# Column groups of 32 in the convolutions, and layer 0's B and C by way of DMA, in a four-layer image kernel

## The chip, the core and the metric

The kernel runs on one core of a Trainium2 chip. The metric is the device time of one execution in microseconds (us); the time before is the median of three runs. A profile of one further execution stands beside it.

## What is computed

The input is a batch of 4 images of 96 channels and 128 x 128 pixels, float32. Four layers follow one another, each as `x = x + layer(group_norm(x))`, with group norms over 32 groups of 3 channels:

- **Layer 0**: a 1x1 projection and a depthwise 3x3 convolution with SiLU give `u`; a second projection gives a gate `z`. Two selective scans with one state each (forward and backward over all 16384 pixels) run over `u`:

```
x_dbl = einsum('bkcl,kdc->bkdl', xs, x_proj_w)      # 6 rows for dt, one for B, one for C
delta = softplus(einsum('bkrl,kcr->bkcl', dts, dt_proj_w) + dt_proj_b)
h = exp(delta*A) * h + delta * u * B ;  y = h * C   # along the pixels
```

  Their sum is normed over the channels, gated with `silu(z)` and projected.
- **Layer 1**: a gated 3x3 convolution of 32 channels, a fractional Fourier path and a Fourier path of 32 channels each, then a dense 3x3 convolution over 96 channels.
- **Layer 2**: a deformable 3x3 convolution: offsets and masks by a 3x3 convolution, then four neighbours gathered for each pixel and tap.
- **Layer 3**: a mask, a 2-D cosine transform, four Mamba blocks (one for each quadrant, 192 inner channels, 16 states), and the transform back.

## The kernel before

**Stages.** For each image there is a *front* (layers 0 and 1 and the offsets of layer 2), a *back* (gathers and sampled convolution of layer 2, head and transform of layer 3), and *layer 3* proper (the scans), then the inverse transform. In time: the front of image 0 alone; then for each image b a stage in which the back of b runs beside the front of b+1 (and beside the inverse transform of b-1), followed by layer 3 of b alone; the last image has its back without a front. Three stages hold both a back and a front.

**Two lanes in one program.** In these stages a planner (class `Program`) records every operation of both lanes and issues them in an order that it works out from costs of its own (`cost`). Each lane is first tried alone (`measure`); an operation's due time there, divided by the lane's length, is its key, and among operations that could start at nearly the same time the lower key goes first. All are issued through one helper, so all their engine instructions stand at line 65 in the profile and their DMAs at line 408. The attribute `pace` scales due times: layer 0's scan sets `self.program.pace = 0.1`, so that this stretch takes up a tenth of its length in the keys, and layer 1 sets it back to 1. Each engine runs its instructions in the order issued, and nearly all DMAs are issued from one queue, SyncE's (SP).

**Layer 0 and layer 1's last convolution** work on blocks of 16 rows (2048 pixels; 8 blocks). `conv9` makes one chunk of 512 pixels: 9 taps, each a float32 matmul of 96 channels in, 96 out, 512 columns, summed in one PSUM tile (tile names `l_pc<-rows,l_wc` in layer 0, `l_p<-rows,l_c` in layer 1). The profile shows each float32 matmul as two MATMUL records. A block is four chunks; in layer 0 each chunk has a tenth matmul, the gate's (`l_pz<-rows,l_winT`). `u` and `silu(z)` go to DRAM planes.

**Layer 0's scan** makes 64 steps an image (32 chunks, two directions). One step: load `uc`; matmul `pd` (delta's argument, `wd`); ACT abs, relu, exp, ln and a DVE add (`l_dl`); matmul `pB` with `wbc`, whose columns all repeat the B row, so that B stands on all 96 partitions of PSUM; ACT exp (`l_dA`); DVE `du = uc * pB`; POOL `du * dl`; DVE scan (`l_h`); matmul `pC` in the same way; DVE `h * pC`. In the second half of the steps there follow the sum of both directions, norm, gate and projection (five more matmuls).

**The back's gathers**: 1152 indirect DMAs an image from POOL (`l_g<-quad_d,l_i`), 128 pixels of 1536 bytes each; each is weighed by two ACT and two DVE operations (`l_sm`, `l_part`), then transposed and multiplied.

**Layer 3** has its order written by its own list scheduler (class `Order`, with costs and keys given by hand). An image is 16 tiles of 48 scans (128 partitions x 512). For each scan: ACT `dA`; matmul `pB` and DVE `dB = du * pB` (one scan of four has its product `dP` from POOL instead, out of lines that a DMA spreads, `l_cl`); DVE scan `l_h`; POOL `hc = h * C` (cost 1.23 in the list); matmul `py` that sums `hc` in PSUM. Each tile has a head: norm, convolution `pu` and gate `pz` (192 channels of two quadrants laid over three tiles of 128; the middle tile, j = 1, holds 64 rows of each quadrant and so takes two matmuls with 64 output columns each), projections, softplus. `T.xq` takes its three leading columns from the tile before, by a DVE copy.

Of the kernel before, what the change touches and what calls it, by code (L numbers as in the profile page):

```python
# [22 lines left out]
F32 = mybir.dt.float32  # L23
# [9 lines left out]
L = H * W  # L33
# [100 lines left out]
class Tile:  # L134


    def __init__(self, shape, make, kind, real=None):
        self.shape, self.make, self.kind, self.real = shape, make, kind, real
        self.ops, self.reads, self.writes = [], [], []
# [58 lines left out]
class Pool:  # L198
# [19 lines left out]
    def tile(self, shape, dtype, name, tag=None, bufs=None):  # L218
        tag = tag or name
        tile = Tile(shape, lambda: self.pool.tile(shape, dtype, name=name, tag=tag, bufs=bufs), self.kind)  # L220
        tiles = self.tags.setdefault(tag, [])
        tile.before = tiles[-1] if tiles else None
        n = bufs or self.bufs
        tile.slot = tiles[-n] if len(tiles) >= n else None
        tiles.append(tile)
        return View(tile)
# [10 lines left out]
class Program:  # L237
# [88 lines left out]
    def touch(self, op, view, write):  # L326
# [11 lines left out]
        t.ops.append(op)  # L338
        p0, p1, f0, f1 = view.region()
# [19 lines left out]
    def cost(self, engine, name, out, ins):  # L359
# [7 lines left out]
        if engine == "PE":  # L367
            return 1.1 * (0.00085 * n if name == "transpose" else max(0.165, 0.005 + 0.001667 * n)), None
# [139 lines left out]
class Net:  # L508
# [32 lines left out]
    def stats_tile(self):  # L541
        return self.small.tile([C, NCH, 6], F32, name="stats", tag="stats", bufs=(1, 3)[self.program.lane])
# [37 lines left out]
    def conv9(self, ps, wt, src, i, g):  # L580
# [3 lines left out]
        r0 = BR * i + 4 * g  # L584
        taps = [(0, 0)] + [(y, x) for y in (-1, 0, 1) for x in (-1, 0, 1) if (y, x) != (0, 0)]
        for n, (y, x) in enumerate(taps):
            ra, rb = max(r0, -y), min(r0 + 4, H - y)
            ca, cb = max(0, -x), min(W, W - x)
            at = ra + y - BR * i + 1
            self.nc.tensor.matmul(  # L590
                out=p3[:, ra - r0 : rb - r0, ca:cb],
                lhsT=wt[:, (y + 1) * 3 + x + 1, :],
                rhs=s3[:, at : at + rb - ra, ca + x : cb + x],
                start=n == 0,
                stop=n == 8,
            )
            if n % 3 == 2:
                yield 2.6
# [22 lines left out]
    def layer0(self, xin, T, beside):  # L621
        nc, a = self.nc, self.a
        u_d, sz_d, part_d = self.plane("u_d"), self.plane("sz_d"), self.plane("part_d")
        st0, T.st1 = self.stats_tile(), self.stats_tile()
        with self.program.pool(name="l0w", bufs=1) as wp, self.program.pool(name="l0p", bufs=1, space=PSUM) as ps:
# [6 lines left out]
            nc.sync.dma_start(out=xpd, in_=a["L0_conv_x_proj_w"][:, 0:R6, :].rearrange("k r c -> r k c"))  # L632
            wc = wp.tile([C, 9, C], F32, name="l0_wc")
# [22 lines left out]
            wd = wp.tile([C, 2, C], F32, name="l0_wd")  # L656
            wbc = wp.tile([C, 4, C], F32, name="l0_wbc")
            for k in range(2):
# [3 lines left out]
                nc.vector.tensor_copy(wd[:, k, :], pw[:C, :C])  # L662
                for n in range(2):
                    nc.vector.tensor_copy(
                        wbc[:, 2 * k + n, :], xpT[:, k, R6 + n : R6 + n + 1].to_broadcast([C, C])
                    )
# [3 lines left out]
            with self.program.pool(name="l0a", bufs=3) as wa, self.program.pool("l3i", 2) as wt:  # L670

                def block(i):
# [5 lines left out]
                    for g in range(4):  # L678
                        s = slice(BR * i * W + g * CH, BR * i * W + (g + 1) * CH)
                        pc = ps.tile([C, CH], F32, name="l0_pc", tag="a", bufs=2)  # L680
                        yield from self.conv9(pc, wc, xb, i, g)
                        u = wa.tile([C, CH], F32, name="l0_u", tag="u")
                        nc.scalar.activation(u, pc, AF.Silu, bias=v[:, 0:1], scale=1.0)
                        nc.sync.dma_start(out=u_d[:, s], in_=u)
                        pz = ps.tile([C, CH], F32, name="l0_pz", tag="b", bufs=1)
                        nc.tensor.matmul(
                            out=pz, lhsT=winT[:, C : 2 * C], rhs=xb[:, W + g * CH : W + (g + 1) * CH],
                            start=True, stop=True,
                        )
                        yield  # L690
                        sz = wa.tile([C, CH], F32, name="l0_sz", tag="sz")
                        nc.scalar.activation(sz, pz, AF.Silu)
                        nc.sync.dma_start(out=sz_d[:, s], in_=sz)

                jobs = [staggered((block(i) for i in range(NB)), 16)]
# [3 lines left out]
            self.program.pace = 0.1  # L699
            with self.program.pool(name="l0b", bufs=3) as wb:  # L700
                edges = [None, None]

                def scan(k, n):
                    t = n if k == 0 else NCH - 1 - n
                    s = slice(t * CH, (t + 1) * CH)
                    uc = wb.tile([C, CH], F32, name="l0_uc", tag="uc", bufs=6)
                    nc.sync.dma_start(out=uc, in_=u_d[:, s])
                    second = n >= NCH // 2
                    if second:
                        xc = wb.tile([C, CH], F32, name="l0_x", tag="x", bufs=4)  # L710
                        nc.sync.dma_start(out=xc, in_=xin[:, s])
                        sz = wb.tile([C, CH], F32, name="l0_z", tag="z", bufs=4)
                        nc.sync.dma_start(out=sz, in_=sz_d[:, s])
                    yield
                    yield
                    pd = ps.tile([C, CH], F32, name="l0_pd", tag="b", bufs=1)
                    nc.tensor.matmul(out=pd, lhsT=wd[:, k, :], rhs=uc, start=True, stop=True)
                    yield
                    dl = wb.tile([C, CH], F32, name="l0_dl", tag="dl")
                    tmp = wb.tile([C, CH], F32, name="l0_tmp", tag="tmp")  # L720
# [6 lines left out]
                    pB = ps.tile([C, CH], F32, name="l0_pB", tag="c", bufs=2)  # L727
                    nc.tensor.matmul(out=pB, lhsT=wbc[:, 2 * k, :], rhs=uc, start=True, stop=True)
# [4 lines left out]
                    nc.vector.tensor_tensor(du, uc, pB, ALU.mult)  # L733
# [18 lines left out]
                    if second:  # L752
                        part = self.load(wb, part_d[:, s], [C, CH], "l0_part", 3)
                    pC = ps.tile([C, CH], F32, name="l0_pC", tag="c", bufs=2)
                    nc.tensor.matmul(out=pC, lhsT=wbc[:, 2 * k + 1, :], rhs=uc, start=True, stop=True)
                    yield
                    nc.vector.tensor_tensor(h, h, pC, ALU.mult)
# [13 lines left out]
                    sq = wb.tile([C, CH], F32, name="cn_s", tag="sq")  # L771
# [4 lines left out]
                    nc.tensor.matmul(out=pv, lhsT=self.cavg, rhs=sq, start=True, stop=True)  # L776
                    yield
                    nc.scalar.activation(sq, pv, AF.Ln, bias=self.eps[:C], scale=1.0)
                    nc.scalar.activation(sq, sq, AF.Exp, scale=-0.5)
                    yield  # L780
                    nc.vector.tensor_tensor(ct, ct, sq, ALU.mult)
# [15 lines left out]
    def layer1(self, T):  # L797
        nc, a = self.nc, self.a
        self.program.pace = 1.0
# [4 lines left out]
        T.st2 = self.stats_tile()  # L804
        with self.program.pool(name="l1w", bufs=1) as wp:
# [13 lines left out]
            cb = self.load(wp, a["l1_vec"], [C, 2], "l1_cb")  # L819
            cb0 = wp.tile([64, 1], F32, name="l1_cb0")  # L820
            for j in range(2):
# [13 lines left out]
            with self.program.pool(name="l1p", bufs=2, space=PSUM) as ps, self.program.pool(  # L835
# [49 lines left out]
                def block(i):  # L885
# [22 lines left out]
                    for g in (0, 2):  # L908
                        at = BR * i * W + g * CH
                        pc = ps.tile([64, 4, W], F32, name="l1_pc", tag="c", bufs=1)  # L910
                        for n, x in enumerate((0, -1, 1)):
                            ca, cb_ = max(0, -x), min(W, W - x)
                            nc.tensor.matmul(
                                out=pc[:, :, ca:cb_], lhsT=w0s[:, x + 1, :],
                                rhs=x4[:, 2 * g : 2 * g + 4, 0, ca + x : cb_ + x],
                                start=n == 0, stop=n == 2,
                            )
                        yield
                        c0 = wm.tile([64, 4, W], F32, name="l1_c0o", tag="c0", bufs=3)
                        nc.scalar.activation(c0, pc, AF.Identity, bias=cb0, scale=1.0)  # L920
                        to = cat_d[0:32, at : at + 8 * W].rearrange("o (r two w) -> o r two w", two=2, w=W)
                        for j in range(2):
                            nc.sync.dma_start(out=to[:, :, j, :], in_=c0[32 * j : 32 * j + 32])
                        yield
                        yield
# [25 lines left out]
            with self.program.pool(name="l1r", bufs=2, space=PSUM) as ps, self.program.pool(name="l1c", bufs=3) as wa:  # L951

                def block2(i):
# [3 lines left out]
                    for g in range(4):  # L957
                        t = 4 * i + g
                        s = slice(t * CH, (t + 1) * CH)
                        xc = self.load(wa, T.x1[:, s], [C, CH], "l1_x")  # L960
                        pc = ps.tile([C, CH], F32, name="l1_p2", tag="a")
                        yield from self.conv9(pc, w2, xb, i, g)
                        nc.vector.scalar_tensor_tensor(xc, pc, cb[:, 1:2], xc, ALU.add, ALU.add)
                        nc.vector.bn_stats(T.st2[:, t, :], xc)
                        nc.sync.dma_start(out=T.x2[:, s], in_=xc)

                yield from staggered((block2(i) for i in range(NB)), 12)
# [745 lines left out]
    def pair_head(self, i, at, T, before, wq, wb, ps, order):  # L1713
# [12 lines left out]
        def load():  # L1726
# [8 lines left out]
            else:  # L1735
                nc.vector.tensor_copy(T.xq[:, :, 0:3], last.xq[:, :, CH : CH + 3])

        o("DVE", 0.2, load, "load",
# [64 lines left out]
        def conv(j, k, q, p, n, ch, first):  # L1803
            if first:
                v.pu[j] = ps.tile([128, CH], F32, name="l3_pu", tag="a")
            nc.tensor.matmul(
                out=v.pu[j][p : p + n, :], lhsT=T.wts[1][:, q, k, ch : ch + n],
                rhs=T.xq[:, q, k : k + CH], start=k == 0, stop=k == 3,
            )

        def gate(j, q, p, n, ch, first):
            if first:
                v.pz[j] = ps.tile([128, CH], F32, name="l3_pz", tag="a")
# [537 lines left out]
```

## Time and profile before

| | |
|---|---|
| median of 3 runs | 15512.11 us (15500.95 to 15518.31) |
| the profiled execution's own time | 15515.38 us |
| its span, first to last instruction | 15513.2 us |
| busy: PE, DVE, POOL, ACT | 84%, 73%, 69%, 58% |
| front of image 0, alone | 0 to 1443 us |
| back 0 with front 1; back 1 with front 2; back 2 with front 3 | 1443 to 3548; 5074 to 7168; 8652 to 10806 |
| layer 3 of images 0, 1, 2, 3 | 3548 to 5074; 7168 to 8652; 10806 to 12272; 13946 to 15424 |
| back 3 (with inverse 2) | 12272 to 13946 |
| inverse 3 | 15424 to 15513 |

Times in the profile are us from the first instruction. A group's line gives its count, busy time and the mean of one in ns, then the time that its engine stood idle before it and what ended that. PE is TensorE's matmuls, PEld its weight loads, which lie beside the matmuls. A row of windows gives, for a stretch, busy time and count for PE, PEld, DVE, ACT and POOL, the granted clock of TensorE, the mean busy share of the DMA engines and the GB/s that they moved.

### The profile page before, as it was taken

What the parts mean: (1) busy time and instruction counts of PE and PEld (TensorE: products, weight loads), DVE (VectorE), ACT (ScalarE), POOL (GpSimd) and SP (SyncE); (2) the same over time, 40 slices, a digit from 0 to 9 for tenths busy, and PEclk for the clock granted to TensorE, in tenths of its full rate; (3) what the DMA queues carried; (4) which work ended last, traced back from release to release, by engine and by line L of the source; (5) the groups of instructions that cost most, each with busy time, mean ns of one, the idle gap of its engine ahead of it and who ended that gap; (6) DMA issues with size and microseconds to landing.
All of it is one profiled execution on the core that took longest, in us unless ns stands there. A gap on an engine that the chain in (4) does not pass through costs nothing. (4 is left out here: it accounts for less than half of the span.)

```text
span 15513.2 us, 158595 instructions
## 1 busy us (share of the span) xinstructions
PE 13036.3 (84%) x38368; PEld 6057.7 (39%) x38368; DVE 11396.8 (73%) x21639; ACT 9043.9 (58%) x21651; POOL 10642.7 (69%) x9472
## 2 busy tenths in 40 slices
PE   8897888889999788898999688888999744459998
PEld 3343334444333334544333343544333322233334
DVE  2725487677999577677999668666999765548997
ACT  2613586556665477555666468555666455546664
POOL 2101756756999664764999774773999877748997
PEclk9998999989999899999999899998999955579999
DMA  3445658776666766876666775976666765556666
GB/s 97 124 127 161 197 160 244 215 220 176 182 188 181 231 196 193 236 223 188 186 185 185 209 224 155 253 212 206 185 185 184 208 178 166 166 150 177 183 189 190
DMA packets 1315541, 2913.63 MB, mean 188 GB/s; under 512 B 271728, under 2 KB 757808, under 8 KB 1200304
## 3 DMA queue, kind: packets, MB, share of 16 engines
q1 hardware_dynamic: 1016240, 1997.11, 44.3%
q0 software_dynamic: 298368, 906.38, 19.8%
q8 instruction: 305, 5.00, 0.1%
q14 instruction: 628, 5.14, 0.1%
HBM read 2455.27 MB, written 447.48 MB: 187 GB/s over the span
## 5 line engine op out<-in xcount | busy, mean ns | idle before, releaser
L65 POOL DMA_INDIRECT l_g<-quad_d,l_i x4608 | 4680.9, 1016 | 2502.4 <-issue 1281.2
L65 POOL TENSOR_TENSOR l_hc<-l_h,l_cl 128x512 f32<-128x512 f32 x3072 | 3829.3, 1273 | 253.0 <-PE l_py L65 167.6
L65 PE MATMUL l_py<-l_hc,ident 128*128 128x512 f32 x6144 | 3076.6, 609 | 46.7 <-POOL l_hc L65 41.5
L65 DVE TENSOR_TENSOR_SCAN l_h<-l_dA,l_carry,l_dB 128x512 f32<-128x512 f32 x2304 | 2860.8, 1268 | 2.3
L65 ACT ACTIVATE l_dA<-l_dl,l_al 128x512 f32<-128x512 f32 x2304 | 1633.9, 718 | 1235.0 <-DVE l_h L65 1220.8
L65 DVE SCALAR_TENSOR_TENSOR l_sm<-l_g,l_v,l_sm 128x96 f32<-128x96 f32 x4608 | 1465.1, 322 | 1109.6 <-ACT l_sm L65 1084.8
L65 ACT ACTIVATE l_sm<-l_g,l_v 128x96 f32<-128x96 f32 x4608 | 1646.7, 369 | 1009.2 <-DMA l_g<-quad_d,l_i 928.4
L65 ACT ACTIVATE l_part<-l_g,l_v 128x96 f32<-128x96 f32 x4608 | 1630.9, 364 | 464.7 <-DVE l_sm L65 463.1
L65 PEld LDWEIGHTS l_py<-l_hc,ident 128*128 128x128 f32 x6144 | 1132.0, 192 | 1313.4 <-issue 838.2
L65 PE MATMUL l_pc<-l_sT,l_wk 128*96 128x256 f32 (+1 forms) x3584 | 1208.5, 456 | 434.4 <-ACT l_sT L65 430.8
L65 DVE TENSOR_TENSOR l_dB<-l_du,l_pB 128x512 f32<-128x512 f32 x2304 | 1503.1, 681 | 83.8 <-PE l_pB L65 47.6
L65 PE MATMUL l_pB<-l_bc,pick 128*128 128x512 f32 x2304 | 1394.8, 629 | 130.6 <-DVE l_dB L65 105.8
L65 DVE SCALAR_TENSOR_TENSOR l_part<-l_g,l_v,l_part 128x96 f32<-128x96 f32 x4608 | 1469.5, 324 | 29.4 <-ACT l_part L65 27.2
L65 PE MATMUL l_pt<-ident,l_sm 128*128 128x128 f32 (+1 forms) x3584 | 779.2, 318 | 793.1 <-DVE l_sm L65 749.2
L65 PE MATMUL l_p<-rows,l_c 96*96 96x508 f32 (+2 forms) x2304 | 1052.1, 597 | 61.5 <-DMA rows<-cat_d 42.5
L65 PE MATMUL l_pc<-rows,l_wc 96*96 96x508 f32 (+2 forms) x2304 | 1062.0, 600 | 30.0 <-DVE rows L65 30.0
L65 PE MATMUL l_pu<-l_xq,l_wc 96*64 96x512 f32 (+1 forms) x2048 | 1040.2, 616 | 27.5 <-ACT l_xq L65 23.5
L65 DVE TENSOR_TENSOR_SCAN l_h<-l_dQ,l_carry,l_dP 128x512 f32<-128x512 f32 x768 | 974.3, 1269 | 116.0 <-POOL l_dP L65 97.6
L65 POOL TENSOR_TENSOR l_dP<-l_du,l_cl 128x512 f32<-128x512 f32 x768 | 978.8, 1274 | 85.1 <-DMA l_cl<-bc_d 60.9
L65 PEld LDWEIGHTS l_pc<-l_sT,l_wk 128*96 128x96 f32 (+1 forms) x3584 | 648.8, 195 | 934.9 <-ACT l_sT L65 532.5
L65 POOL TENSOR_TENSOR l_du<-l_du,l_dl 96x512 f32<-96x512 f32 x256 | 336.8, 1316 | 986.6 <-DVE l_dl L65 579.1
L65 PEld LDWEIGHTS l_pt<-ident,l_sm 128*128 128x128 f32 (+1 forms) x3584 | 519.6, 161 | 1170.8 <-DVE l_sm L65 708.9
(265 smaller groups left out, 20011.1 us busy)
## 6 DMA issues: line engine op xcount, KB each, us to landing
l_cl<-bc_d SPq DMA_DIRECT2D x512, 1280.0 KB
l_cl<-bc_d SPq DMA_DIRECT2D x512, 640.0 KB
quad_d<-l_qt SPq DMA_DIRECT2D x124, 768.0 KB
x<-l_x SPq DMA_DIRECT2D x384, 192.0 KB
l_g<-quad_d,l_i POOLq DMA_INDIRECT x4608
l_uc<-u_d SPq DMA_DIRECT2D x256, 192.0 KB
l_x<-x SPq DMA_DIRECT2D x256, 192.0 KB
l_xs<-x SPq DMA_DIRECT2D x116, 256.0 KB
```

Of the source, the lines that this page charges most:

```text
L65: ins = op(*args, **kw).ins
```

## The change

1. `conv9` and layer 0's gate matmul take the four chunks of a block in three rounds. A round r fills a PSUM tile of 128 partitions: three groups of 32 partitions hold the output channels 0-31, 32-63, 64-95 of chunk r, the fourth holds channels 32r to 32r+31 of chunk 3. So each tap is four matmuls with 32 output columns each, on four column groups, instead of one of 96. What follows (bias, SiLU, adding, statistics) works on 128 partitions and three times a block, not four; each store or load of such a tile is two DMAs. Layer 1's small convolution puts two chunks side by side (64 + 64 columns) in the same way.
2. In layer 0's scan `wd` has two more columns, B and C, so `pd` has 98 rows. ACT copies the two rows out, a DMA writes them to DRAM, another reads them back spread over 96 partitions (`lines`), and the two DVE products take their operand from SBUF. The matmuls `pB` and `pC` go. `pd` has two PSUM buffers, not one; `uc`, `x`, `z`, `part`, `tmp` have one buffer less each; `z` and `x` are loaded later.
3. `pace` is 1 throughout.
4. The planner: matmuls with up to 32 or 64 rows out cost a quarter or a half (over 256 columns); an operation on a tile whose buffer has already been given to a later tile makes that one wait.
5. Layer 3: POOL's `hc` takes two scans at once (128 x 1024); the two halves of `pu` and `pz` for j = 1 are issued next to each other; the copy of three columns into `xq` goes from DVE to ACT, but for the first tile of a quadrant pair.

```diff
@@ conv9
+    def shares(r):
+        return [(32 * j, r, 32 * j) for j in range(3)] + [(C, 3, 32 * r)]
+    def spread_out(self, dst, t, i, r):
+        at = BR * i * W
+        self.nc.sync.dma_start(out=dst[:, at + r * CH : at + (r + 1) * CH], in_=t[:C])
+        self.nc.sync.dma_start(out=dst[32 * r : 32 * r + 32, at + 3 * CH : at + 4 * CH], in_=t[C:])
...
+            for p, g, c in self.shares(r):
+                r0 = BR * i + 4 * g
...
+                self.nc.tensor.matmul(
+                    out=p3[p : p + 32, ra - r0 : rb - r0, ca:cb],
+                    lhsT=wt[:, (y + 1) * 3 + x + 1, c : c + 32],
@@ layer0, convolution
-                    for g in range(4):
-                        pc = ps.tile([C, CH], F32, name="l0_pc", tag="a", bufs=2)
-                        yield from self.conv9(pc, wc, xb, i, g)
+                    for r in range(3):
+                        pc = ps.tile([128, CH], F32, name="l0_pc", tag="a", bufs=2)
+                        yield from self.conv9(pc, wc, xb, i, r)
@@ layer0, scan
-            self.program.pace = 0.1
...
-                    pd = ps.tile([C, CH], F32, name="l0_pd", tag="b", bufs=1)
+                    pd = ps.tile([C + 2, CH], F32, name="l0_pd", tag="c", bufs=2)
+                    bc = wb.tile([2, CH], F32, name="l0_bc", tag="bc", bufs=2)
+                    nc.scalar.copy(bc, pd[C:])
+                    nc.sync.dma_start(out=bc_d[2 * k : 2 * k + 2, s], in_=bc)
...
-                    nc.tensor.matmul(out=pB, lhsT=wbc[:, 2 * k, :], rhs=uc, start=True, stop=True)
+                    lines = wb.tile([C, 2, CH], F32, name="l0_lines", tag="lines", bufs=3)
+                    nc.sync.dma_start(
+                        out=lines, in_=bc_d[2 * k : 2 * k + 2, s].unsqueeze(0).to_broadcast([C, 2, CH])
+                    )
-                    nc.vector.tensor_tensor(du, uc, pB, ALU.mult)
+                    nc.vector.tensor_tensor(du, uc, lines[:, 0, :], ALU.mult)
...
-                    nc.tensor.matmul(out=pC, lhsT=wbc[:, 2 * k + 1, :], rhs=uc, start=True, stop=True)
-                    nc.vector.tensor_tensor(h, h, pC, ALU.mult)
+                    nc.vector.tensor_tensor(h, h, lines[:, 1, :], ALU.mult)
@@ layer 3
-                nc.vector.tensor_copy(T.xq[:, :, 0:3], last.xq[:, :, CH : CH + 3])
+                nc.scalar.copy(T.xq[:, :, 0:3], last.xq[:, :, CH : CH + 3])
...
+            for q, p, n, ch in self.PARTS[j]:
+                nc.tensor.matmul(
+                    out=v.pu[j][p : p + n, :], lhsT=T.wts[1][:, q, k, ch : ch + n],
...
-                    nc.gpsimd.tensor_tensor(v.hc, v.h[:, r % 2, :], v.cl[:, s % NS, :], ALU.mult)
+                    v.hc = wb.tile([128, 2, CH], F32, name="l3_hc", tag="hc", bufs=LAG // 2)
+                    rows = slice(0, NS, 3) if r == 1 else slice(1, 3)
+                    nc.gpsimd.tensor_tensor(v.hc, v.h, v.cl[:, rows, :], ALU.mult)
...
-                main("HC", n, "POOL", 1.23, hc, 1.5, ("SC", n), ("CL", g), ("HC", n - 1), ("PY", n - LAG))
+                    main("HC", n, "POOL", 2.27, hc, 1.5, ("SC", n), ("CL", g), ("HC", n - 2), ("PY", n - LAG))
```

## The prediction, made before the change was run

> **What bounds the kernel now.** I read first the busy time by stage. The columns are busy us and count for PE, PEld, DVE, ACT, POOL, then clock, DMA share, GB/s: front 0 alone, back 1 with front 2, back 3 with no front, and a piece of layer 3.
>
> ```profile
> 0.00:1443.00 1443.00, 1257.68 (x3650) 564.36 (x3650) 619.33 (x1140) 488.17 (x989) 150.01 (x176) 0.95 0.43 121
> 5074.00:7168.00 2094.00, 1781.89 (x6344) 928.25 (x6344) 1450.80 (x3859) 1298.19 (x3668) 1306.52 (x1241) 0.92 0.73 216
> 12272.00:13946.00 1674.00, 800.69 (x2712) 504.58 (x2710) 927.56 (x2756) 890.27 (x2678) 1169.82 (x1191) 0.62 0.59 172
> 14000.00:15400.00 1400.00, 1341.72 (x3128) 525.04 (x3128) 1328.02 (x1467) 903.29 (x1681) 1312.70 (x1065) 0.99 0.64 186
> ```
>
> Front 0 is PE's. Layer 3 has PE, DVE and POOL all at 94 to 96%. In the mixed stage nothing is full, so I cut it by what POOL's gathers do (rows of `l_g` alone), beside the whole stretches of the scan (in the stage, and in front 0) and of the gathers alone:
>
> ```profile
> 5074.00:5650.00 576.00, 406.43 (x408) 0.88 0.77 230
> 5650.00:6030.00 380.00, 108.04 (x95) 0.94 0.52 156
> 6030.00:6925.00 895.00, 658.85 (x638) 0.92 0.82 235
> ...
> 5650.00:6030.00 380.00, 331.13 (x759) 121.95 (x759) 345.28 (x541) 323.32 (x693) 184.01 (x153) 0.94 0.52 156
> 330.00:690.00 360.00, 318.64 (x709) 112.90 (x709) 296.77 (x402) 294.65 (x547) 83.99 (x64) 0.97 0.40 122
> 12290.00:13766.00 1476.00, 664.02 (x2157) 428.33 (x2157) 858.33 (x2646) 831.96 (x2581) 1118.80 (x1152) 0.59 0.60 178
> ```
>
> Alone, 1152 gathers take 1476 us: 1.281 each, and POOL takes no more. In the convolution stretch (408 x 1.281 = 523 of 576) and later (817 of 895) the stage runs at nearly that pace. In layer 0's scan 95 gathers run where 297 would fit: 380 - 122 = 258 us lost. After the last gather come 243 us of head, transform and offsets. So a mixed stage is 1468 of gathers + 53 + 258 + 78 lost + 237 of tail = 2094.
>
> Last, TensorE's pace, from the timeline, and layer 3's chain:
>
> ```profile
> 102.72 7.85 PE L65 MATMUL l_pc<-rows,l_wc 96*96 96x512 f32 x18
> 110.41 1.02 PE L65 MATMUL l_pz<-rows,l_winT 96*96 96x512 f32 x2
> 3701.99 1.07 PE L65 MATMUL l_pu<-l_xq,l_wc 96*64 96x512 f32 x2
> 11049.07 1.08 PE L65 MATMUL l_pu<-l_xq,l_wc 96*64 96x512 f32 x4
> by line: PE l_py L65 22.7%; PE l_pu L65 12.1%; DVE l_h L65 12.1%; issue 10.4%; PE l_pB L65 6.1%; POOL l_hc L65 5.0%; DVE l_dB L65 4.8%; PE l_po L65 3.5%; DMA l_xc<-xd_d 3.2%; DMA l_cl<-bc_d 2.7%; POOL l_dP L65 2.4%; PE l_pz L65 2.2%; ACT l_
> ```
>
> 18 records start over 110.41 - 102.72 = 7.69 us: 0.427 each, 0.854 a float32 matmul. The last two timeline rows carry the change: four records on two column halves, each with its own moving data, end in the time of two.
>
> **Convolutions.** A block's nine taps are 36 matmuls now and 27 rounds of four afterwards; with the gate, 40 and 30. Four at once is not in the trace, two at once is. Bounds for a round: 0.854 (like the pair) and 1.708 (only two share). I take 0.854, since the pair shows no loss at all; both ends go into the range. Front 0: the convolution stretch, 8 x 40 x 0.854 = 273 us (it lasts 273, 57 to 330), becomes 8 x 30 x 0.854 = 205: -68. Layer 1's last convolution, 246 of the 260 us from 985 to 1245, becomes 184: -61. The evictions fall from four to three a block. Weight loads quadruple in number; one of 64 columns takes 132 ns, four of 32 at that price 0.53 in a round of 0.854, hidden beside the matmuls; without that cover a few us a block. The DMAs rise from four to six a block and tensor (64 more an image, 0.30 us each on SP as for `l_uc<-u_d`), 19 us on a queue that is not the bound. I allow 9 us for all this: front 0 -120.
>
> A rule speaks against this. The Trainium skill, "TensorE: Matmul & The Clock Gate", section "Part 3: Packing small matmuls", gives 2.38x for three column tiles and 3.07x for four row tiles, not 3 and 4. A round would then be 4 x 0.854/3.07 = 1.11 us and the convolutions would gain 12 us an image, not 129; the time would be some 15,400. The row of the pair shows no such loss.
>
> **Layer 0's scan.** Out go 128 matmuls an image: 109 us of PE. In come, for each of 64 steps, an ACT copy of 2 x 512 from PSUM (nearest rows: `l_carry`, 0.18, and `l_ct<-l_pm`, 0.57; length and not partitions should decide, so 0.57: +36), a store and a spread load on SP (128 x 0.30 = 38 us of issue) with 393 KB each (25 MB an image; the stretch has a DMA share of 0.40 to 0.52). DVE's two products lose their PSUM operand: 0.665 before; `l_dl<-l_dl,l_tmp`, both in SBUF, has a median of 0.686 and a mean of 0.820: +3 to +20. Alone, the stretch goes from PE's 319 of 360 us to ACT's 295 + 36 = 331: between 330 and 395; I take 360, no change. What is new is a trip through DRAM between `pd` and `du`; one way (`uc` issued 327.6, its matmul 330.5) is 2.9 us, two are 5.8, about a step (360/64 = 5.6). It is not on the recurrence, so steps ahead hide it; but on SP the load waits for the store, and behind it queue the next steps' `uc`, `part` and x1's stores. That price lies between 0 and 64 x 2.9 = 186 us an image; I take 0.
>
> "VectorE: DVE Perf Modes", section "Two Vector instructions with no wait between them", says that an operation with two SBUF inputs reads one of them through an interface shared with GpSimd; by it the upper price, 20 us, is the one. The mean of 0.820 against 0.665 agrees.
>
> **Gathers beside the scan.** With `pace` at 1 the scan holds 360 of some 1320 us of the front's keys, 27%; the gathers fill 89% of the back's (1476/1656): 1152 x 0.27/0.89 = 350 of them fall to it, in place of 95. ACT gives each 832/1152 = 0.722, DVE 858/1152 = 0.745. The stretch then needs ACT 331 + 253 = 584, DVE 310 + 261 = 571, POOL 84 + 448 = 532. Today's best engine there is at 345/380 = 91%, so 584/0.91 = 642 us, with 448 of gathers in it: 194 lost, not 258. The rest: PE has 109 + 129 = 238 us less of 1782, and fewer gathers stand beside the convolutions; that gives the losses of 53 and 78 some back, I say 36 together. Per stage -64 - 36 = -100 (ends: all 258 + 131 lost but the scan's own 84 of POOL: -300; if ACT and DVE block each other in the scan: +40). Three stages: -300.
>
> **Layer 3.** Of a tile's 203 PE records (3248 in the stage, 16 tiles) ten go, since the pairs of j = 1 share: 4.3 us of 88. DVE loses its copy of three columns (13 in 1400 us, mean 1283 ns: 1.2 us a tile); ACT takes it at about 0.18. POOL's pairs: bounds are two times 1.275 and one time 1.275; near the first, I take 2.45, 2.4 us a tile. PE has about half of the chain, so 5% less of it is 2.4%, and DVE's copy 0.2 us: 2.3 us a tile, 37 an image, with POOL's share 40. Ends: +60 (see below) and -80. Four images: -160. Back 3 and inverse 3: 0.
>
> **Sum.** -120 - 300 - 160 = -580 from the profiled execution's 15,515, which lies 3 us above the median: 14,930.
>
> **Rivals.**
>
> - *The scan gives nothing back, layer 3 neither.* ACT, DVE and SP fill the scan, every gather there costs what it saves, and DVE stays the limit of layer 3. For: ACT and DVE come out above 90%. Against: POOL stands idle for half of that stretch. Front 0 alone: 15,390.
> - *It works better.* Gathers run through the scan at their own pace: -250 a stage, layer 3 -65 an image, front 0 -130: 14,380.
> - *Slower: four column groups don't share.* Two by two, a round is 1.708: front 0 +259 where I have -129, and a mixed stage has PE at 1782 - 109 + 259 = 1932, bound by PE at 2094 to 2300, +100. In all +259 + 300 - 160 = +400: 15,910. It decides from a round of about 1.2 us (580 us over 4 x 456 rounds, 0.32 more each). Against it: the pair's row.
> - *Slower: POOL's double `hc`.* `dP` and the heads queue behind 2.45 us, not 1.275. The scan on `dP` waited 45 times for 26 us in 1400. If each of 768 waits 1.2 us more, +922 and no gain: 16,020; it decides from 0.55 us each. Against it: `dP` is made a group ahead, into two buffers.
>
> **How the numbers follow.** Forecast 0.50 (own range 14,700 to 15,200); nothing back 0.17; better 0.15; column groups 0.08; `hc` 0.06; about no change 0.04. From 14,400 to 15,420 leaves out some of the better case and the slower ones: 2 in 10. Faster by over 0.2% (31 us, about what a measurement can tell here): 0.50 + 0.17 + 0.15 = 0.82; within it 0.03; slower 0.15.
>
> **What would show it.** Right: convolution stretch of front 0 about 205 us, its rounds of eight records in 1.0; gathers in layer 0's scan over 300 in some 640 us; mixed stages near 2000; layer 3's tile near 86. Wrong: rounds above 1.2 us; PE or DVE in the scan waiting for `lines`; `l_h` waiting for `l_dP` beyond 0.5 us each; a tail after the gathers longer than 243.

## The result, and the profile after

The changed kernel takes 15,576.64 us (median; 15,559.58 to 15,600.24), 1.0043 of the kernel before (95% interval 1.0028 to 1.0057): slower by 65 us, where 14,930 was forecast. The profiled execution spans 15,574.6 us, 61.4 more than before. By stage, in us (a mixed stage and back 3 go from the first gather of their image to the first matmul of its layer 3):

| stage | before | after | forecast change | measured |
|---|---|---|---|---|
| front 0 alone | 1445 | 1345 | -120 | -100 |
| three mixed stages | 2106, 2108, 2117 | 2191, 2249, 2247 | -100 each | +85, +141, +130 |
| back 3 | 1654 | 1656 | 0 | +2 |
| layer 3, four images, to the next stage | 1511, 1510, 1496, 1566 | 1454, 1459, 1452, 1521 | -40 each | -57, -51, -44, -45 |

Front 0 and layer 3 came near their forecasts. Nearly the whole miss is in the mixed stages: 356 us longer, where 300 us shorter were forecast. The stage windows of the changed kernel (us, then busy us and count for PE, PEld, DVE, ACT and POOL, granted clock, DMA share, GB/s) answer to the first four of before: front 0, back 1 with front 2, back 3, layer 3 of image 3.

```profile
0.00:1345.00 1345.00, 1066.44 (x5826) 538.33 (x5826) 622.86 (x1122) 517.32 (x1029) 166.14 (x176) 0.86 0.52 149
4990.00:7240.00 2250.00, 1842.71 (x8521) 828.80 (x8522) 1449.61 (x3857) 1315.34 (x3710) 1371.71 (x1250) 0.88 0.75 216
12398.00:14053.00 1655.00, 792.29 (x2694) 504.31 (x2694) 923.49 (x2748) 891.66 (x2676) 1164.79 (x1186) 0.62 0.59 174
14053.00:15485.00 1432.00, 1319.27 (x3234) 536.68 (x3235) 1347.65 (x1516) 941.94 (x1758) 1289.69 (x706) 0.98 0.65 187
```

In front 0 PE has 191 us less than before. In the mixed stage it has 61 us *more* (1843 against 1782), where 238 less were forecast: the same matmuls cost more there than alone. The two convolution stretches of that stage (layer 0's and layer 1's) say it plainer; first before, then after:

```profile
5126.00:5584.00 458.00, 404.82 (x1467) 212.16 (x1467) 259.43 (x833) 269.49 (x852) 338.98 (x342) 0.93 0.77 232
6507.00:6846.00 339.00, 323.50 (x1003) 151.82 (x1004) 224.91 (x691) 183.76 (x600) 256.55 (x253) 0.98 0.72 213
```

```profile
5069.00:5514.00 445.00, 443.40 (x2506) 141.51 (x2510) 197.50 (x620) 200.44 (x628) 272.44 (x271) 1.00 0.67 200
6593.00:6942.00 349.00, 348.99 (x2002) 98.66 (x2002) 154.17 (x474) 122.55 (x415) 194.17 (x196) 0.99 0.58 170
```

Before, PE was busy 728 of 797 us and 593 gathers ran between their first and last convolution matmuls. Now PE is busy 792 of 794, at a granted clock of 0.99 to 1.00, and only 467 run. TensorE is the bound: 126 gathers fewer gave the two stretches back 3 us. What happens in them is in PE's timeline (start, length, operation, records):

```profile
5200.33 1.04 PE L65 MATMUL l_pc<-rows,l_wc 96*32 96x508 f32 x2
5201.30 0.44 PE L65 MATMUL l_pt<-ident,l_sm 128*128 128x128 f32 x2
5201.67 1.05 PE L65 MATMUL l_pc<-rows,l_wc 96*32 96x508 f32 x6
5202.65 1.16 PE L65 MATMUL t_p<-k_dct,t_in 128*128 128x128 f32 x8
5203.74 1.07 PE L65 MATMUL l_pz<-rows,l_winT 96*32 96x512 f32 x8
5204.62 1.04 PE L65 MATMUL l_pc<-rows,l_wc 96*32 96x512 f32 x8
5205.59 0.67 PE L65 MATMUL l_pc<-l_sT,l_wk 128*96 128x256 f32 x2
```

A round is here four matmuls, one on each column group, or eight records; nine rounds fill a PSUM tile. The first row has two of them (one matmul), the third six, the sixth all eight, and each holds the array for 0.97 or 0.98 us, from its start to that of the next row. A matmul of 32 columns that is alone costs as much as four together. The planner, which records each matmul singly and at a quarter of the cost, puts the other lane's `l_pt`, `t_p` and `l_pc<-l_sT` inside the groups: a run of two or of six records is a round that was split. From start to start, a record of these convolutions took 107 to 108 ns in front 0, where there is no other lane, but 171 ns here for layer 0's convolution (with the gate) and 163 for layer 1's; between the other lane's matmuls they stood in 199 and 150 runs, 137 and 110 of these of two or four records. That makes a round 1.37 us (329 us over 240) and 1.30 us (281 over 216), not 0.854. Before, the records of 96 columns lost little in the same stage: 446 and 454 ns, against 430 in front 0.

The scan's stretch, in the stage and alone in front 0:

```profile
5445.00:6025.00 580.00, 394.37 (x1266) 170.69 (x1266) 441.65 (x966) 455.09 (x1150) 430.01 (x347) 0.75 0.77 216
257.00:640.00 383.00, 260.98 (x413) 76.41 (x410) 286.19 (x354) 322.26 (x586) 97.64 (x63) 0.69 0.57 174
```

From the first to the last of DVE's `l_du` it is now 574 us with 297 gathers (371 with 88 before). Alone it is 370 us, 324 before, while PE's busy time and clock fell (row `330.00:690.00` of before: 319 us, 0.97).

The stage's 141 us are then: 3 less in the convolutions, 203 more in the scan, 54 more in the tail after the last gather (240 to 294), and 113 less in what is left, with 83 gathers fewer in it.

### The profile page after: what moved, and what is told of

It is laid out like the page before. It is cut to its first block, busy times and chain, and to the rows that moved or that the text cites. A ratio compares the mean times of both kernels' runs of the same rounds, so it can differ in the third digit from the quotient of the medians.

```text
span 15574.6 us, 174101 instructions
## 1 busy us (share of the span) xinstructions
PE 12717.0 (82%) x47072; PEld 5695.3 (37%) x47072; DVE 11310.7 (73%) x21511; ACT 9118.8 (59%) x21865; POOL 10588.8 (68%) x7936
## 4 chain that ended last, share of the span: by engine, by line
PE 33%; POOL 15%; DMA 11%; issue 7%; DVE 7%; ACT 4%; SPq 1%; POOLq 0%; DVEq 0%; ACTq 0%
PE l_py L65 8%; POOL l_g L65 6%; PE l_pc L65 5%; POOL l_hc L65 5%; DMA l_g<-quad_d,l_i 4%; PE l_pu L65 4%; PE l_p L65 4%; DVE l_h L65 3%; PE l_po L65 2%; PE t_p L65 2%; PE l_pB L65 2%; POOL l_dP L65 2%; DMA l_cl<-bc_d 1%; PE l_pt L65 1%; PE l_pz L65 1%
## 5 line engine op out<-in xcount | busy, mean ns | idle before, releaser
L65 POOL DMA_INDIRECT l_g<-quad_d,l_i x4608 | 4818.3, 1046 | 2826.4 <-issue 1226.8
L65 POOL TENSOR_TENSOR l_hc<-l_h,l_cl 128x1024 f32<-128x1024 f32 x1536 | 3614.4, 2366 | 283.9 <-DVE l_h L65 251.7
L65 PE MATMUL l_pc<-l_sT,l_wk 128*96 128x256 f32 (+1 forms) x3584 | 1312.7, 481 | 459.2 <-ACT l_sT L65 450.7
L65 PE MATMUL l_pt<-ident,l_sm 128*128 128x128 f32 (+1 forms) x3584 | 873.0, 339 | 798.9 <-DVE l_sm L65 758.5
L65 PE MATMUL l_pc<-rows,l_wc 96*32 96x508 f32 (+3 forms) x6912 | 1148.4, 598 | 21.5 <-DVE rows L65 21.5
L65 PE MATMUL l_p<-rows,l_c 96*32 96x508 f32 (+3 forms) x6912 | 1066.8, 598 | 39.0 <-DMA rows<-cat_d 24.5
L65 DVE TENSOR_TENSOR_SCAN l_h<-l_dQ,l_carry,l_dP 128x512 f32<-128x512 f32 x768 | 972.0, 1266 | 61.0 <-POOL l_dP L65 56.8
L65 ACT COPY l_sT<-l_pt 128x512 f32<-128x512 f32 (+1 forms) x1024 | 524.1, 522 | 634.7 <-PE l_pt L65 633.6
L65 PEld LDWEIGHTS l_pB<-l_bc,pick 128*128 128x128 f32 x2304 | 436.2, 190 | 1060.7 <-DVE l_dB L65 839.0
```

The lines of the kernel that those rows point to most:

```text
L65: ins = op(*args, **kw).ins
```

## The experiments

Three theories stood at first. **Theory 1**: the other lane's matmuls split the groups of four. **Theory 2**: even keys, that is gathers beside the scan, cost more than they give. **Theory 3**: the trip of B and C over ScalarE, DRAM and SyncE's queue costs it. Runs of one group shared a chip. On three of the four chips the gathers were slower: back 3's 1152 took 1694 to 1730 us where the first profiles show 1469 and 1471, and the kernel before took 16,881, 17,029 and 17,003 us. So ratios are compared within a group, and stage times only between chips alike. The edits are shown shortened.

**First group (kernel before: 16,881 us).** Groups kept together: the twelve matmuls of three taps, and the gate's four, are one operation of the planner, with the sum of their costs.

```diff
-                yield from (nine taps, each matmul an operation of its own)
+        for m in range(0, 9, 3):
+            with self.program.together():      # recorded as one operation
+                for n in range(m, m + 3): ... the four matmuls of tap n
+            yield 2.6
```

> The changed kernel, with the twelve matmuls of three taps (and the four of the gate) recorded as one operation of the planner, so that the other lane's matmuls cannot come between column groups. Theory 1 (the other lane's matmuls split the groups of four, so that they no longer share the array): in the mixed stages a conv record falls from 0.16-0.18 us to about 0.11, 200 us of PE a stage come free, the stages fall from 2190-2250 to 2000-2100, the time to 15,000-15,250. Theory 2 (the loss comes from the even keys: gathers beside the scan of layer 0 stretch it and starve the rest): the stages stay above 2180, the time above 15,450.

0.980 (0.9774 to 0.9826).

The scan's keys pressed into a tenth again, alone:

```diff
+            self.program.pace = 0.1      # ahead of layer 0's scan
+        self.program.pace = 1.0          # at the start of layer 1
```

> The changed kernel with the pace of 0.1 in layer 0's scan put back, and nothing else. Theory 1: the conv records in the mixed stages still cost 0.16 us or more, the convolution stretches stay bound by PE, and the time is 15,450 or more. Theory 2: the stages fall below the 2107 that they took before, the time to 15,000-15,250.

0.9986 (0.997 to 1.0002).

Both edits:

> Both: three taps as one operation, and the pace of 0.1 put back. Theory 1: about as glue3 (within 100 us), since the pace was not what cost. Theory 2: below glue3 by 200 us or more, and near pace. If both count: below either, under 15,000.

1.0034 (1.0019 to 1.0048).

The kernel before with even keys alone (and with the changed planner's wait for a buffer that has been given on):

```diff
-            self.program.pace = 0.1
-        self.program.pace = 1.0
```

> The kernel before, with the pace at 1 throughout (and the planner's wait for late users of a buffer, without which this order stops): gathers beside the scan, but convolutions of 96 columns and B and C by matmuls. Theory 1: no split groups, so no loss: 15,300 to 15,550, stages of 2040 to 2120. Theory 2: the even keys alone cost 60 to 120 us a stage: 15,700 to 15,850.

0.9852 (0.9832 to 0.9873). Theory 2 falls: even keys by themselves make the kernel before 1.5% faster, and taking them from the kernel with kept groups costs 2.4%. Keeping groups brings nothing under pressed keys (1.0034 against 0.9986), which none of the theories expected. The trace of the run with pressed keys alone shows one reason: the rounds are hardly split there. In back 1 with front 2 its convolutions stand in 93 and 58 runs, 23 of them of two or four records; with even keys it was 199 and 150 runs, 247 of them so short. The changed kernel itself was not run on this chip, so the 0.980 says only that the edit with even keys beats the kernel before.

**Second group (kernel before: 15,517.72 us, a chip like the first).** The changed kernel again:

> The changed kernel as it is, beside the others. All theories: within 1% of the kernel before, mixed stages 60 to 140 us longer than before's, front 0 100 us shorter, layer 3 40 to 50 us an image shorter.

1.0052 (1.0035 to 1.0069), stages 2208, 2249, 2252.

All 36 matmuls of a PSUM tile, nine rounds of four, as one operation (`range(0, 9, 9)` in the edit above; below, the kernel with kept rounds; the expectations call all 36 a round):

> The changed kernel with all 36 matmuls of a round as one operation of the planner. Theory 1 (split groups): the conv records in the mixed stages cost 0.11 us, 2 to 4% faster than the changed kernel. Theory 2 (even keys, crowded scan): within 0.5% of the changed kernel. Against both: long operations (8 us) keep the other lane's transposes waiting, gathers slow down, slower.

15,031.58 us, 0.9688 (0.9671 to 0.9704): 3.6% below the unedited change, faster than both kernels. The stages are 1990, 2068, 2066. Its timeline and the same two stretches:

```profile
5003.64 1.16 PE L65 MATMUL t_p<-k_dct,t_t 128*128 128x128 f32 x8
5004.73 7.89 PE L65 MATMUL l_pc<-rows,l_wc 96*32 96x512 f32 x72
5012.55 0.67 PE L65 MATMUL l_pc<-l_sT,l_wk 128*96 128x256 f32 x2
```

```profile
4869.00:5183.00 314.00, 287.88 (x2356) 121.82 (x2356) 175.08 (x570) 185.03 (x586) 236.01 (x233) 0.95 0.78 235
6324.00:6561.00 237.00, 236.40 (x1988) 93.44 (x1988) 146.06 (x449) 110.56 (x377) 177.60 (x179) 0.99 0.80 236
```

72 records in 7.82 us are nine rounds of 0.87; PE is busy 524 us instead of 792 in the two stretches, which last 551 instead of 794. The other lane's records are cheaper too: in layer 1's convolution `l_pc<-l_sT` takes 229 ns from start to start, not 296, and `l_pt` 125, not 200. In that stage the convolutions' records take 110 ns from start to start, as theory 1 had it. Theory 1 is shown.

The convolutions and the gate back in 96 columns and four chunks, the rest of the change kept:

```diff
-                    for r in range(3): ... conv9(pc, wc, xb, i, r)   # 4 x 32 columns
+                    for g in range(4): ... conv9(pc, wc, xb, i, g)   # 96 columns
```

> The changed kernel with the 3x3 convolutions of layers 0 and 1 and the gate's matmul back at 96 columns and four chunks a block. Theory 1: front 0 loses its 129 us, but each mixed stage gains 60 to 120 since nothing is split and no tiling mode is changed: 0.3 to 1.5% faster than the changed kernel. Theory 2: only the loss in front 0 and in PE's load: 1 to 2.5% slower than the changed kernel.

0.9849 (0.9832 to 0.9865), front 0 at 1473, stages 2063, 2107, 2108. Beside the repeat of the change, the column groups win 126 us in front 0 and lose 142 to 145 in each mixed stage; without them the change is 1.5% faster than before, not 0.5% slower. That is 2.0% faster than the changed kernel, more than the 0.3 to 1.5% that theory 1 gave it.

The scan as before, with `pB` and `pC`, keys even, the rest of the change kept:

```diff
-                    nc.scalar.copy(bc, pd[C:]); store to bc_d; load lines
+                    nc.tensor.matmul(out=pB, lhsT=wbc[:, 2 * k, :], rhs=uc, start=True, stop=True)
```

> The changed kernel with layer 0's scan as before (B and C spread by matmuls), the pace still 1. Theory 1: the scan is not the cause: front 0 gains the 47 us that its scan lost, stages within 40 us. Theory 3 (the trip of B and C over ACT, DRAM and SP is what costs in the stages): each scan stretch 60 to 120 us shorter, 1.5 to 2.5% faster than the changed kernel.

0.9907 (0.9891 to 0.9924): front 0 is 45 us shorter than in the repeat of the change, the stages 60, 53 and 56. The gain of 1.4% falls between the theories: theory 1 allowed 40 us a stage, theory 3 asked for 60 to 120 in each scan, where the scans of the mixed stages gained 30 to 52. The scan as before also brings back its buffers and its earlier loads; the third group separates the trip from them. Theory 3 holds, as the smaller cause.

**Third group (kernel before: 17,028.6 us): why the scan alone got longer.** Either the clock (0.69) or the trip. Two matmuls a step that nobody reads give PE its old work; a load from the image in place of the lines just stored takes only the wait of load on store away (B and C are then other numbers):

```diff
+                    nc.tensor.matmul(out=pw, lhsT=wd[:, k, :C], rhs=uc, start=True, stop=True)  # twice
```

> The kernel with the 36 matmuls kept together, B and C still by the trip through DRAM, and two further 96x512 matmuls a step of layer 0's scan whose result nobody reads: TensorE has the work that it had in the scan before. Theory 'clock' (the scan alone got longer, 324 to 372 us, because TensorE has little to do there and its granted clock fell from 0.97 to 0.69, so that every matmul on the way of a step takes longer): the scan of front 0 comes back to 325 to 340 us at a clock over 0.9, front 0 to about 1315, the total to 14,990 or less. Theory 'trip' (the way over ScalarE, DRAM and SyncE's queue sets the pace): the scan stays at 372 or gets longer, the total at 15,030 to 15,150.

```diff
-                        out=lines, in_=bc_d[2 * k : 2 * k + 2, s].unsqueeze(0).to_broadcast([C, 2, CH])
+                        out=lines, in_=xin[2 * k : 2 * k + 2, s].unsqueeze(0).to_broadcast([C, 2, CH])
```

> The kernel with the 36 matmuls kept together, whose two lines a step are loaded from the image instead of from the lines just stored: copy, store, load and products stay, in number and in bytes, only the load no longer has to wait for the store (so B and C are wrong values). Theory 'trip': the scan of front 0 falls from 372 to 325 to 340 us, the mixed stages by some 40 each, the total to some 14,870. Theory 'clock', or the theory that the added instructions and bytes themselves cost it: the scan stays at 365 to 375 and the total at 15,000 to 15,040.

With the idle matmuls 0.9812 (0.9791 to 0.9833), without the wait 0.9724 (0.9705 to 0.9743). Windows of the scan in front 0, first with the idle matmuls, then without the wait:

```profile
257.00:640.00 383.00, 326.30 (x655) 110.07 (x650) 279.75 (x349) 317.41 (x575) 98.08 (x62) 0.90 0.58 172
```

```profile
257.00:640.00 383.00, 251.66 (x456) 77.21 (x456) 330.82 (x409) 335.00 (x611) 101.16 (x64) 0.77 0.64 184
```

With the clock back at 0.90 the scan still takes 378 us from first to last `l_du`. Without the wait it takes 331, all instructions and bytes in place, at a clock of 0.77. On the same chip the scan with the trip as it was took 365 us in the next run, and the scan by matmuls 326 in the last run of this group. The trip is the cost and the clock is not: 34 of 39 us are the wait of load on store.

Only the four matmuls of one tap together (`range(0, 9, 1)`):

> The changed kernel with only the four matmuls of one tap kept as one piece of the order, so that the other lane's matmuls may come between two taps (up to 9 pieces a round, not 1). If it is enough that the four of a tap stay together, the time is that of the 36 kept together, 0.969 of the kernel before. If each change from one lane's matmuls to the other's costs by itself, the gain is a part of it: by the number of changes, 0.98 to 0.995.

0.9769 (0.975 to 0.9787); the kernel with 36 has 0.9777 in the fourth group, on another chip. Both have slow gathers, and as the end of this section shows such a chip can't tell them apart; on a chip with fast gathers four at a time was not tried. So whether four are enough stays open.

Kept rounds together with the scan as before:

> The changed kernel with a block's 36 convolution matmuls kept as one piece of the order, and with layer 0's scan as before (B and C by matmuls). If the two costs are separate, their gains add: front 0 from 1354 to about 1305, each mixed stage from some 2067 to 2020, 15,030 - 49 - 3 x 45 = 14,850, 0.957 of the kernel before. The rival: the scan's matmuls come back as work of a TensorE that the kept rounds have just relieved, and in the mixed stages nothing is won; then 14,980 to 15,050, 0.966 to 0.970.

0.9671 (0.9653 to 0.969). That lies in the rival's band, but both bands were worked out for fast gathers. Its stages (2424 to 2479 us) stand on slow ones, so the fourth group repeats it beside its base.

**Fourth group (kernel before: 17,003 us).** Kept rounds, kept rounds with the scan as before, kept rounds with pressed keys:

> The kernel with the 36 matmuls of a round kept as one piece of the order, once more, beside the two that differ from it by one part: 0.969 of the kernel before on a chip whose gathers alone take some 1470 us a stage, 0.975 to 0.985 on one where they take 1700.

0.9777 (0.9753 to 0.9802).

> The same with layer 0's scan as before (B and C by matmuls), beside it on one chip. If the trip's cost in the mixed stages is what it is in front 0 alone (41 to 49 us), the stages fall by 40 to 50 from those of the kernel with the trip (to about 2020 where that has 2067) and the total by 180 to 200 us. If the gathers hide it there (POOL is theirs, and the trip's waits are filled with them), only front 0 gains: 45 to 60 us in all.

0.9674 (0.9643 to 0.9705), 180 us less by the spans: 42 in front 0, and 6, 71 and 59 in the stages. The trip costs in two of the three mixed stages too. This is the best version on the chips with slow gathers; on a fast one it was not run.

> The same as the first of these three, with the line that presses layer 0's scan into a tenth of its keys put back, so that few gathers run beside the scan. If gathers beside the scan are worth what the prediction gave them (64 us a stage or more), the total is 200 to 400 us longer than that of the first. If the scan gives nothing back, the two agree within 60 us.

0.9997 (0.9978 to 1.0017): 343 us more by the spans, 201, 98 and 76 in the stages. So even keys do pay, by more than the 64 us a stage of the prediction, but here with gathers of 1.5 us each.

**What the chips with slow gathers don't show.** There the convolutions of the mixed stages are no shorter with kept rounds. In back 1 with front 2 the two stretches together take 883 us with kept rounds (551 on the fast chip), 898 and 915 with three taps and one tap together, and 869 in the changed kernel with pressed keys. The kernel with kept rounds in the fourth group, its two stretches and a piece of PE's timeline:

```profile
5279.00:5780.00 501.00, 424.46 (x2357) 150.19 (x2356) 174.44 (x563) 182.69 (x580) 246.56 (x249) 0.82 0.54 156
7044.00:7426.00 382.00, 333.28 (x1990) 114.03 (x1991) 149.49 (x458) 117.03 (x401) 184.88 (x187) 0.87 0.53 151
```

```profile
5417.40 3.91 PE L65 MATMUL l_pc<-rows,l_wc 96*32 96x512 f32 x29
5421.69 1.34 PE L65 MATMUL l_pc<-rows,l_wc 96*32 96x508 f32 x3 [0.37 <-issue]
5423.86 0.59 PE L65 MATMUL l_pc<-rows,l_wc 96*32 96x508 f32 x1 [0.84 <-issue]
```

The order is the same as on the fast chip, 33 and 23 runs, but PE stands idle inside a kept run, and the profile names no cause ("issue"): a record of layer 0's convolution takes 221 ns from start to start, not 110. Nor is it the pace of the gathers: 436 in 883 us are 2.0 us each, where alone they take 1.5. What holds PE up there is open. So theory 1 rests on the second group, and what the kept rounds win was seen on its chip alone.

## Why the prediction was wrong

**The step that failed** is in "Convolutions": "I take 0.854, since the pair shows no loss at all". The pair is layer 3's, whose order is written by hand and runs alone; front 0 has only one lane as well. There the step is right (conv stretches 275 to 207 and 248 to 186 us, forecast 273 to 205 and 246 to 184); front 0 came out at -100, since its scan took 46 us more and its other parts some 16 less. The prediction then carried it into stages whose order a planner makes out of single matmuls of two lanes, where a round is 1.30 to 1.37 us. Its term "PE has 109 + 129 = 238 us less of 1782" became +61. Its slower rival had the price ("decides from a round of about 1.2 us") but the wrong mechanism and place: four groups do share; they are not left together.

That took the next step down with it. The prediction gave "fewer gathers stand beside the convolutions" 36 us with the shorter PE; in fact 126 fewer gathers gave 3 us, because PE had become the bound there. In the same stage the scan took 209 more gathers for 203 us more, and the 83 gathers taken out of the rest gave 113 back. That exchange, one side paid and the other in part, with the 54 us of tail, is the mixed stage's loss. The tail goes with the even keys, not with the split: it is 234 to 250 us in the four kernels with pressed keys, the one before among them, and 250 to 337 in all with even ones, kept rounds too (250 to 277). The prediction kept it at its old length; why it grows was not looked into.

**The scan's trip**, between 0 and 186 us an image, was taken at 0 ("It is not on the recurrence, so steps ahead hide it"). It costs 38 to 46 us in the scan alone, and taking it out gains 53 to 60 a stage on the fast chip, 6 to 71 on the slow one. In the code `du` stands one `yield` after the load, half of the distance between two steps. SyncE waited 65.7 us for the copy ahead of the store in front 0's scan, and DVE's `du` waited for the lines:

```profile
SPq L419 <- ACT l_bc L65: 65.7, 50, 4.0
...
DVE l_du L65 <- DMA l_lines<-l0bc_d: 25.9, 20, 2.7
```

Without the dependence the scan recovers though the store still waits (38.7 us). So it is mostly the time from store to lines, not the queue's blocking, that is paid.

**Gathers beside the scan**: forecast 350 in place of 95, in 642 us in place of 380: 262 us for 255 more, 1.03 us each, -64 a stage. The changed kernel paid 203 us for 209, 0.97 each; with kept rounds it was 296 in 567, 196 us for 208, 0.94 each, the trip's cost included. The mechanism was right and the price nearly so. With both costs gone a stage is 2068 - 53 = 2015 by the second group (the sum of two edits, not run together on such a chip), where 2000 was forecast.

**The Trainium skill's** 3.07x for four row tiles, in "TensorE: Matmul & The Clock Gate", section "Part 3: Packing small matmuls", would by the prediction's estimate have made a round 1.11 us in front 0 too. There it is 0.86, nearly the full four times (a record of 96 columns took 430 ns, one of a round 107 to 108), so the row of the pair was the better guide. But no row of the trace of before showed column groups between another lane's matmuls. The 15,400 that the prediction names for that round is not the sum of its own terms: front 0 would lose 117 of its 120, the mixed stages at most 3 x 36, which makes some 15,150. Its being nearer to the measured time would have been luck.

**Layer 3** gained 44 to 57 us an image, 40 forecast. POOL's pair took 2.366 us (forecast 2.45), and the wait that the fourth rival feared fell; the scan on `dP` before, then after, with POOL's pair:

```profile
L65 DVE TENSOR_TENSOR_SCAN l_h<-l_dQ,l_carry,l_dP 128x512 f32<-128x512 f32 x768 | 974.3, 1269 | 116.0 <-POOL l_dP L65 97.6
...
L65 POOL TENSOR_TENSOR l_hc<-l_h,l_cl 128x1024 f32<-128x1024 f32 x1536 | 3614.4, 2366 | 283.9 <-DVE l_h L65 251.7
...
L65 DVE TENSOR_TENSOR_SCAN l_h<-l_dQ,l_carry,l_dP 128x512 f32<-128x512 f32 x768 | 972.0, 1266 | 61.0 <-POOL l_dP L65 56.8
```

The wait is 56.8 us in the whole kernel, 97.6 before.

Of the signs of being wrong, three of four came true: "rounds above 1.2 us", DVE "waiting for `lines`" (the row above) and "a tail after the gathers longer than 243" (265 to 297). Rounds had to be looked for in the mixed stage: front 0's were fine.

## What to carry to other kernels

Matmuls that share the array by column groups are one piece of work: give the scheduler the whole group, not its members at a quarter of the cost, or another stream's matmul may split it, and here each part then cost nearly as much as the whole. Measure the gain on more than one chip. A price measured where an engine serves one stream must be checked against how the order is made where it serves two. When work is moved from a stretch to another, ask what bounds the stretch that it leaves: it gives nothing back if another engine is full there.

## What the runs showed of the hardware

- A run of two, six or eight records on column groups of 32 held TensorE for 0.97 to 0.98 us before another tile shape; within a long run a round took 0.86 to 0.87.
- TensorE's granted clock in layer 0's scan fell to 0.69 when 128 of its matmuls went, and `l_pd` rose from 624 to 912 ns; 128 idle matmuls brought 0.90 and 674 ns back and won no time (378 us of scan, not 365).
- POOL's `du * dl` slowed when the operand of DVE's products moved from PSUM to SBUF, and came back with it. That fits what the Trainium skill, "VectorE: DVE Perf Modes", section "Two Vector instructions with no wait between them", says of a DVE operation with two SBUF inputs: it reads one of them through an interface shared with GpSimd. DVE's own products went from 0.664 to 0.676 us (`du`) and from 0.674 to 0.760 (`h * C`). The clock is not the reason, since POOL's product took 1.58 us with the idle matmuls too; the DMA that writes `lines` came and went with the operand, so that rival is left. The scan in front 0, of the changed kernel and of the one with kept rounds and the scan as before:

```profile
L65 POOL TENSOR_TENSOR l_du<-l_du,l_dl 96x512 f32<-96x512 f32 x63 | 99.0, 1571 | 450.8 <-DVE l_du L65 265.8 <-DMA l_lines<-l0bc_d 185.0
```

```profile
L65 POOL TENSOR_TENSOR l_du<-l_du,l_dl 96x512 f32<-96x512 f32 x64 | 83.2, 1300 | 419.4 <-DMA l_uc<-u_d 176.2 <-DVE l_dl L65 167.2 <-DVE l_du L65 76.0
```

- Chips differ: back 3's gathers took 1.27 to 1.28 us each in the first profiles and on the second group's chip, and 1.47 to 1.50 on three others. The same kernel took 0.9688 of the time before there and 0.9777 here.
